# Layer 3's group (1,0): half of its depthwise convolution from VectorE to TensorE, with three small tiles put into one ring

## The chip, the cores and the metric

The kernel runs on one NeuronCore of a Trainium2 chip. TensorE (PE) multiplies matrices, VectorE (DVE) and ScalarE (ACT) work element by element, GpSimd (POOL) does small element work and issues indirect DMAs, SyncE (SP) issues the other DMAs. Each engine runs its own instructions in order, and waits for others by semaphores. The metric is the device time of one execution in microseconds; lower is better.

## The reference, cut to what matters

The input x is 16 images of 192 channels and 32x32 pixels. Four layers each add something to x: `x = x + layer(groupnorm(x))`, with 32 groups of channels.

- Layer 0 is an mLSTM block with a convolution (the kernel's phase A).
- Layer 1 is an attention whose scores come from small simulated quantum circuits: per head a state vector of 64 amplitudes goes through two fixed matrices, and its squares give queries and keys.
- Layer 2 computes offsets with a 3x3 convolution, samples x at the offset positions (9 taps, bilinear), and weights the taps by channel.
- Layer 3 is the one that the change is about:

```
h  = einsum('bchw,oc->bohw', x, w_in)             # 192 -> 510 channels
h  = irfft2(rfft2(2x2 patches of h) * fft_w)      # 2x2 spectral weights
d  = depthwise 3x3 convolution, 510 -> 1020 channels (two outputs per input channel), padding 1
x1, x2 = d[:, :510], d[:, 510:]
y  = einsum('bchw,oc->bohw', gelu(x1) * x2, w_out)
```

## The kernel before

**Phases.** Phase A (layer 0) is one long stage. Phase B holds layers 1 to 3 and the end of layer 0. It is written as five generators that a helper `weave` interleaves by costs that the generators yield: `vectors` (state vectors of layer 1), `attention`, `offsets` and `gathers` (layer 2), and `layer3`. The streams run staggered over the 16 images, so that at any time several images are under way. A scheduler then orders the instructions of each engine, and buffers of a tag are reused in turn (a ring), so that a tile waits until the last reader of the tile that had its buffer is done.

**Layer 3.** The 510 channels are two halves, ab = 0 and 1 (the result of ab=0, `dv[0]`, goes through GELU; that of ab=1, `dv[1]`, is the factor), each in two parts of 128, gt = 0 and 1. For each gt, `rows_in` makes the input rows with TensorE (`phad`, line 1523) and combines them on VectorE into `g.pad` (line 1535); `planes` forms the sums and differences of neighbouring columns, `oe` (line 1571) and two more planes of `pad` (lines 1577 and 1580). Then for eo = 0, 1, the two outputs of an input channel, comes the depthwise convolution, for both ab. So there are eight groups (ab, gt, eo).

A group on VectorE goes by `step`: 12 taps over four planes (a fast form of the 3-tap row filter), of which the first two are ScalarE's (line 1598), ten are VectorE's (line 1600), and between them are one subtraction (line 1616) and one more step (line 1618). A group on TensorE goes by `conv`: for each of the two column halves, nine matrix products of `oe` with diagonal 128x128 matrices (`g.dtaps`, one for each tap; line 1561), summed in PSUM (`pdc`), and one ScalarE eviction (line 1563). `onpe` says for which (gt, eo) the half ab=1 goes to TensorE: (0,0) for images 0 to 13; all four pairs for the last two images. Then come the GELU (ScalarE, line 1625), the product with the other half (line 1627), the output product `pout` (line 1639), and `total`, which loads the residual into `xo` (line 1630), adds (line 1632) and stores (line 1633).

**The diagonal matrices** of (0,0) are built at phase B's start, nine ScalarE instructions on the identity matrix; those that are missing for the last two images are built at image 14, into borrowed `v4` buffers (line 1548).

**Small tiles.** `psit` is a ring of two 2 KB buffers for transposed state vectors `psiT` (line 1084; read by `pcirc`, line 1091). `xp` is a ring of two 2 KB buffers for `ot` (line 1392, offsets), `x2` (lines 1448 to 1457, residual of layer 2) and `xo`. `pos`, `fi`, `fl`, `iv` (lines 1399 to 1417) are single buffers for sampling positions, from which the gather indices `ix` come. `mr` and `mp` (lines 1227 to 1232) are single buffers for row maxima of the attention, which go through DRAM (`mxd`) into `qT`.

Of the kernel before, what the change touches and what calls it, by code (L numbers as in the profile page):

```python
# [10 lines left out]
F32 = mybir.dt.float32  # L11
I32 = mybir.dt.int32
BF16 = mybir.dt.bfloat16
AF = mybir.ActivationFunctionType
ALU = mybir.AluOpType
# [6 lines left out]
HS = 512  # L22
# [782 lines left out]
def phase_b(tc, d, out, ydram, stats, cn, nb):  # L805

    nc = tc.nc
    with ExitStack() as ctx:
# [20 lines left out]
        def sb(tag, bufs, n=HW):  # L829
            return lambda name: p2.tile([128, n], F32, tag=tag, name=name, bufs=bufs)  # L830

        v4, e4, u4 = sb("v4", 5), sb("e4", 3), sb("u4", 3)
        u8 = sb("u8", 2, 2048)
        psit, xp, u384 = sb("psit", 2, HS), sb("xp", 2, HS), sb("u384", 2, 384)

        def pairs(name):
            return p2.tile([128, 2, 192], F32, tag=name, name=name, bufs={"acc": 3, "xt": 2}[name])
# [25 lines left out]
        nc.sync.dma_start(boff, d["b_off"].partition_broadcast(128).rearrange("q n o -> q (n o)"))  # L863
        nc.vector.tensor_tensor(gridb, gridb, boff.unsqueeze(1).to_broadcast([128, 8, 18]), ALU.add)

        wdw = wp.tile([128, 24, 4], F32, name="wdw")
        nc.sync.dma_start(wdw[:, :, 0:3], d["w_dw"].rearrange("p (n x) -> p n x", x=3))
        nc.vector.tensor_copy(wdw[:, :, 3], wdw[:, :, 2])
        wraw = wp.tile([128, 24, 3], F32, name="wraw")
        nc.vector.tensor_copy(wraw, wdw[:, :, 0:3])  # L870
        dtaps = {}
        for gt, eo in ((0, 0),):
            t = wp.tile([128, 9, 128], F32, name=f"dtap{gt}{eo}")
            dtaps[gt, eo] = [t[:, i, :] for i in range(9)]
            for i in range(9):
                nc.scalar.activation(t[:, i, :], cn.ident, AF.Copy,
                                     scale=wraw[:, ((2 + gt) * 2 + eo) * 3 + i // 3, i % 3:i % 3 + 1])
        wa, wb, wc, wd = (wdw[:, :, i] for i in range(4))
        nc.vector.tensor_add(wc, wa, wd)
        nc.vector.tensor_add(wb, wb, wc)  # L880
# [113 lines left out]
def vectors(g, b, left):  # L994
# [82 lines left out]
    for pr in range(3):  # L1077
        ps = []
        for hf in range(2):
            pt = mm("ppsi")  # L1080
            for j in range(4):
                nc.tensor.transpose(pt[:, j * 128:(j + 1) * 128], psi[:, hf * 4 + j, :], cn.ident)
            ps.append(g.psit("psiT"))
            nc.scalar.activation(ps[hf], pt, AF.Identity)
            yield 2.0
        prob = {}
        for w in range(2):
            for hf in range(2):

                pc = big("pcirc")  # L1090
                beside(g.tc, [lambda hh=hh, r=slice(hh * 64, hh * 64 + 64): nc.tensor.matmul(
                    pc[:, hh * HS:(hh + 1) * HS], cn.lqk[r, w, :], ps[hf][r, :], start=True, stop=True)
                    for hh in range(2)])
                prob[w, hf] = v4("prob")
                nc.scalar.activation(prob[w, hf], pc, AF.Square)  # L1095
                yield 2.0

        pz = mm("pz")
        for hh in range(2):
            o = 20 - (pr * 2 + hh) * 4  # L1100
            beside(g.tc, [lambda w=w, hf=hf, q=(w * 2 + hf) * 32: nc.tensor.matmul(
                pz[q:q + 32, :], g.amat[:, w, o:o + 32], prob[w, hf][:, hh * HS:(hh + 1) * HS],
                start=(hh == 0), stop=(hh == 1)) for w in range(2) for hf in range(2)])
        yield 3.0
        if pr == 0:
            nc.scalar.activation(zr, pz, AF.Identity, bias=g.projb)
        else:
            nc.vector.tensor_tensor(zr, zr, pz, ALU.add)
        if pr < 2:
            psi = products(pr + 1)  # L1110
        yield 2.0
# [46 lines left out]
def attention(g):  # L1158
# [14 lines left out]
    def largest(i):  # L1173


        b, pr = pairs[i]
        assert g.done[1] > b
        parts, vo = left[b].parts, g.vo[i % 2]
        kT, qT = g.kt_[i % 2], g.qt_[i % 2]
        xn = g.v4("xn")[:64]  # L1180
        for n, c in ((64, heads[pr][0] * 32),) if pr < 2 else ((32, 64), (32, 160)):
            nc.sync.dma_start(xn[(c == 160) * 32:(c == 160) * 32 + n], g.xnd[b, c:c + n, :])
        for hh in range(2):
            h, o = heads[pr][hh], hh * 64
            for j in range(3):
                key = parts[:, j, 0:480].rearrange("p (t h c) -> p t h c", t=8, h=6)[:, :, h, :]
                diff = parts[:, j, 480:600].rearrange("p (t h c) -> p t h c", t=4, h=6)[:, :, h, :]
                nc.scalar.copy(g.kp[:, :, o:o + 45].rearrange("p t (i j c) -> p t i j c", i=3, j=3)[:, :, :, j, :],
                                      key[:, :, 5:10].unsqueeze(2).to_broadcast([128, 8, 3, 5]))
                nc.scalar.copy(g.kdp[:, :, o:o + 45].rearrange("p t (i j c) -> p t i j c", i=3, j=3)[:, :, :, j, :],  # L1190
                                      diff.unsqueeze(2).to_broadcast([128, 4, 3, 5]))
                nc.scalar.copy(g.qp[:, :, o:o + 45].rearrange("p t (i j c) -> p t i j c", i=3, j=3)[:, :, j],
                                      key[:, :, 0:5].unsqueeze(2).to_broadcast([128, 8, 3, 5]))
        yield 2.0
        rows_of(g.kp, kT)
        rows_of(g.kdp, g.kd)
        rows_of(g.qp, qT)
        yield 3.0
        pv = g.mm("pv").rearrange("p (t h e) -> p t h e", t=8, h=2)
        for tt in range(8):  # L1200
            nc.tensor.transpose(pv[:, tt].rearrange("p h e -> p (h e)"), xn[:, tt * 128:(tt + 1) * 128],
                                cn.ident[:64, :64])
        nc.scalar.activation(vo, pv.rearrange("p t h e -> p t (h e)"), AF.Copy, scale=row("gate"))
        yield 2.0
        mx = p2.tile([128, 2, 8], F32, tag="mx", name="mx")
        for tt in range(8):
            pd, pm = None, None
            for src in (g.kd, kT):
                pm = big("pmax")
                beside(g.tc, [lambda hh=hh, r=slice(hh * 64, hh * 64 + 64): nc.tensor.matmul(  # L1210
                    pm[:, hh * HS:(hh + 1) * HS], qT[r, tt * 128:(tt + 1) * 128], src[r, 0:HS],
                    start=True, stop=True) for hh in range(2)])
                if pd is None:
                    pd, up = pm, e4("up")
                    nc.scalar.activation(up, pd, AF.Relu)  # L1215
                    yield 1.2
            for hh in range(2):
                s = slice(hh * HS, (hh + 1) * HS)
                nc.vector.tensor_tensor_reduce(up[:, s], pm[:, s], up[:, s], 1.0, -3e38, ALU.add, ALU.max,  # L1219
                                               mx[:, hh, tt:tt + 1])  # L1220
            yield 1.2

        yield 1.2
        yield 1.2
        pm = g.mm("pmq")
        nc.tensor.transpose(pm[:16, 0:128], mx.rearrange("p h t -> p (h t)"), cn.ident)
        mr = p2.tile([16, 128], F32, tag="mr", name="mr", bufs=1)
        nc.scalar.activation(mr, pm[:16, 0:128], AF.Identity, scale=-1.0)
        mp = p2.tile([16, 3, 128], BF16, tag="mp", name="mp", bufs=1)
        thirds(nc.vector, mr, [mp[:, j, :] for j in range(3)])  # L1230
        for hh in range(2):
            nc.sync.dma_start(g.mxd[i, hh].rearrange("j (t n) -> t j n", t=8), mp[hh * 8:hh * 8 + 8])
        for hh in range(2):
            nc.sync.dma_start(qT[hh * 64 + 45:hh * 64 + 48, :], g.mxd[i, hh])
        yield 1.0
# [104 lines left out]
def layer2_offsets(g, b, left):  # L1340
# [55 lines left out]
        nc.tensor.transpose(pf[:, j * 128:(j + 1) * 128], ot[:, j * 128:(j + 1) * 128], cn.ident)  # L1396
    yield 4.0
    n = 144
    pos = p1.tile([128, n], F32, tag="pos", name="pos")
    pfv = pf.rearrange("p (j k f c) -> p k f j c", j=4, k=2, f=2)  # L1400
    posv = pos.rearrange("p (f j c) -> p f j c", f=2, j=4)
    nc.vector.tensor_tensor(posv, pfv[:, 0, :, :, 0:18], g.gridb.rearrange("p (f j) c -> p f j c", f=2), ALU.add)
    nc.vector.tensor_tensor(posv, pfv[:, 1, :, :, 0:18], posv, ALU.add)
    nc.vector.tensor_scalar(pos, pos, -1.0, 32.0, ALU.max, ALU.min)
    fi = p1.tile([128, n], I32, tag="fi", name="fi")
    nc.vector.tensor_copy(fi, pos)
    fl = p1.tile([128, n], F32, tag="fl", name="fl")
    nc.vector.tensor_copy(fl, fi)
    t1 = p1.tile([128, n], F32, tag="fi", name="t1")
    nc.vector.tensor_tensor(t1, fl, pos, ALU.is_gt)  # L1410
    nc.vector.tensor_sub(fl, fl, t1)
    nc.vector.tensor_sub(pos, pos, fl)
    flv = fl.rearrange("p (n c) -> p n c", c=2)
    iv = p1.tile([128, n // 2], F32, tag="iv", name="iv")
    nc.vector.scalar_tensor_tensor(iv, flv[:, :, 0], 34.0, flv[:, :, 1], ALU.mult, ALU.add)
    ix = p2.tile([128, n // 2], I32, tag="ix", name="ix")
    nc.vector.tensor_scalar_add(ix, iv, 35.0)
# [66 lines left out]
def layer3(g, b, left):  # L1484
# [99 lines left out]
    for gt in range(2):  # L1584
# [6 lines left out]
        for eo in range(2):  # L1591
# [8 lines left out]
                    nc.vector.scalar_tensor_tensor(out, src, w, add, ALU.mult, ALU.add)  # L1600

            half = [[dv[ab][:, c * HS:(c + 1) * HS] for c in range(2)] for ab in range(2)]
            onpe = (gt, eo) in (((0, 0), (0, 1), (1, 0), (1, 1)) if last else ((0, 0),))
            abs_ = range(1) if onpe else range(2)
            for dy in range(3):
                if onpe and dy:
# [180 lines left out]
```

## Time and profile before

| | |
|---|---|
| median of 3 runs | 7750.31 us (7744.7 to 7766.25) |
| the profiled execution's own time | 7759.77 us |
| its span | 7758.0 us |
| granted TensorE clock, mean of the span | 0.915 |
| busy: TensorE, VectorE, ScalarE, GpSimd | 86%, 81%, 55%, 34% of the span |
| L1600, the tap steps on VectorE | 1060 instructions, 778.2 us |
| L1561, the products of `conv` | 792 instructions, 362.7 us |
| chain that ended last, shares of the span | DVE 21%, PE 15%, issue 11%, DMA 7%, POOL 4%, ACT 3% |

A row of a group reads: line, engine, operation, output<-inputs, shape, count | busy time, mean ns of one | idle time of the engine before it and what ended most of it. A row of waits reads: engine, instruction and line that waited <- what it waited for: microseconds in total, times, longest. A row of the windows view reads: the stretch, its length, then busy microseconds (and instructions) of PE, of its weight loads (PEld), DVE, ACT and POOL, then the granted TensorE clock, the DMA engines' share and GB/s. An f32 matrix product stands in the trace as two instructions.

### The profile page before, as it was taken

To read this page: it belongs to the slowest core of one execution; us is meant where nothing else is said; L and a number is where in the kernel's file an instruction comes from. 1 tells how busy PE (TensorE), PEld (TensorE's weight loads), DVE (VectorE), ACT (ScalarE), POOL (GpSimd) and SP (SyncE) were. 2 spreads that over 40 slices of the span, in tenths; PEclk is the share of its full clock that TensorE was granted. 3 is DMA by queue.
4 is the path that set the end of the run, shared out by engine and by line. 5 is a ranking of instruction groups with operands and counts; after the bars stand their busy time and mean duration, and the time that the engine had idled before them with its cause. 6 is when DMAs were issued, how large, how long until landed. Compare 5 with 4: busy or idle time off the path is not lost.

```text
span 7758.0 us, 94726 instructions
## 1 busy us (share of the span) xinstructions
PE 6690.9 (86%) x32360; PEld 3024.9 (39%) x32360; DVE 6304.9 (81%) x13587; ACT 4301.3 (55%) x7578; POOL 2640.8 (34%) x2125
## 2 busy tenths in 40 slices
PE   6999999999999994788787888888788888877768
PEld 3555555555555552223233333233233323323233
DVE  8888888888888883357887988998898798888886
ACT  6555555555555452766665665666566566556422
POOL 0111111111111110034645545554554565555562
PEclk9999999999999997898998989998899898888878
DMA  1111111111111112045454455545445444544452
GB/s 63 48 50 46 50 50 52 50 47 55 50 47 51 50 44 57 24 132 172 129 154 148 141 151 162 160 147 151 145 142 155 145 153 150 157 147 131 149 169 80
DMA packets 266577, 815.81 MB, mean 105 GB/s; under 512 B 49579, under 2 KB 129725, under 8 KB 266091
## 3 DMA queue, kind: packets, MB, share of 16 engines
q0 software_dynamic: 92160, 453.06, 19.0%
q1 hardware_dynamic: 173931, 356.69, 14.4%
q8 instruction: 254, 4.16, 0.2%
q14 instruction: 232, 1.90, 0.1%
HBM read 667.33 MB, written 133.88 MB: 103 GB/s over the span
## 4 chain that ended last, share of the span: by engine, by line
DVE 21%; PE 15%; issue 11%; DMA 7%; POOL 4%; ACT 3%; SPq 0%; POOLq 0%; DVEq 0%; ACTq 0%; another core or an unknown queue 0%
DVE dc L1600 4%; DMA gt<-xg,ix 3%; DVE up L1219 3%; DVE gt L1469 3%; PE pav L1250 3%; POOL gt L1438 3%; PE pdc L1561 2%; DVE acc L1472 2%; PE pdef L1478 2%; PE phad L1523 2%; DVE acc L1474 2%; POOL df L1360 1%; PE poffc L1386 1%; PE pscore L1257 1%; DVE gnst L32 1%
## 5 line engine op out<-in xcount | busy, mean ns | idle before, releaser
L1438 POOL DMA_INDIRECT gt<-xg,ix x1152 | 1911.6, 1659 | 1911.2 <-DVE acc L1472 1225.9
L529 POOL COPY qbd<-qT 32x384 f32<-32x384 f32 x512 | 318.5, 622 | 2544.2 <-PE se L561 2442.5
L1261 ACT ACTIVATE pexp<-pscore 128x1024 f32<-128x1024 f32 x768 | 783.7, 1022 | 411.9 <-PE pscore L1257 358.1
L1250 PE MATMUL pav<-pexp,vo 128*32 128x512 f32 x3072 | 884.4, 657 | 18.2 <-ACT pexp L1261 8.2
L1469 DVE SCALAR_TENSOR_TENSOR gt<-gt,w 128x384 f32<-128x384 f32 x1152 | 724.1, 645 | 216.0 <-DMA gt<-xg,ix 212.9
L1250 PE MATMUL pav<-pexp,ones 128*32 128x512 f32 x3072 | 891.5, 656 | 0.0
L1600 DVE SCALAR_TENSOR_TENSOR dc<-pad,wdw,dc 128x512 f32<-128x512 f32 x1060 | 778.2, 776 | 19.9 <-ACT dc L1598 19.2
L1478 PE MATMUL pdef<-acc,ident 128*128 128x384 f32 x1152 | 582.7, 597 | 221.9 <-DVE acc L1474 215.2
L1219 DVE CUSTOM_DVE_ANT_0 up<-pmax,up 128x512 f32<-128x512 f32 x768 | 500.1, 684 | 191.0 <-PE pmax L1210 143.2
L1215 ACT ACTIVATE up<-pmax 128x1024 f32<-128x1024 f32 x384 | 391.5, 1019 | 259.8 <-PE pmax L1210 226.4
L559 ACT ACTIVATE dm<-dm,wtm 128x128 f32<-128x128 f32 x1536 | 491.1, 388 | 76.7 <-DVE dm L515 49.9
L1472 DVE SCALAR_TENSOR_TENSOR acc<-gt,w 128x192 f32<-128x192 f32 x1152 | 462.9, 435 | 4.3 <-PE pdef L1478 4.1
L570 PEld LDWEIGHTS pintra<-v,pt 128*128 128x128 f32 x3072 | 390.6, 192 | 169.5 <-issue 104.3
L1257 PE MATMUL pscore<-qt,kt 64*128 64x512 bf16 x1536 | 332.3, 413 | 101.3 <-DVE mx L1219 36.1
L570 PE MATMUL pintra<-v,pt 128*128 128x33 f32 x3072 | 383.6, 271 | 5.2 <-DVE pt L565 4.8
L1478 PEld LDWEIGHTS pdef<-acc,ident 128*128 128x128 f32 x1152 | 200.5, 212 | 458.7 <-DVE acc L1474 304.0
L1561 PE MATMUL pdc<-oe,dtap 128*128 128x496 f32 (+3 forms) x792 | 362.7, 604 | 6.6 <-DVE oe L1571 6.6
L1474 DVE TENSOR_TENSOR acc<-acc,wdef 128x384 f32<-128x384 f32 x576 | 329.9, 573 | 0.3
L1360 POOL TENSOR_TENSOR df<-xpad 96x324 f32<-96x324 f32 x144 | 185.7, 1289 | 413.5 <-issue 333.4
L565 DVE SCALAR_TENSOR_TENSOR pt<-se,dm 128x512 f32<-128x512 f32 x384 | 262.8, 684 | 77.4 <-PE se L561 75.2
L606 PE MATMUL pconv<-yt,wc 128*128 128x512 f32 x640 | 311.5, 607 | 5.3 <-DVE yt L496 2.2
L1523 PE MATMUL phad<-had,win 96*128 96x256 f32 x1024 | 294.7, 434 | 11.6 <-ACT prob L1095 6.6
(444 smaller groups left out, 14066.3 us busy)
## 6 DMA issues: line engine op xcount, KB each, us to landing
dm<-gd SPq DMA_DIRECT2D x128, 768.0 KB
xg<-xt SPq DMA_DIRECT2D x288, 192.0 KB
gt<-xg,ix POOLq DMA_INDIRECT x1152
xb<-x_in SPq DMA_DIRECT2D x32, 384.0 KB
y<-ydram SPq DMA_DIRECT2D x32, 384.0 KB
x1d<-xb SPq DMA_DIRECT2D x32, 384.0 KB
xnd<-y SPq DMA_DIRECT2D x32, 384.0 KB
x<-x1d SPq DMA_DIRECT2D x32, 384.0 KB
```

Of the source, the lines that this page charges most:

```text
L559: nc.scalar.activation(dm[:, h, :], dm[:, h, :], AF.Exp, bias=wtm[:, c, 64 + h:65 + h])
L570: nc.tensor.matmul(pa[:, hh * 33:hh * 33 + 33], pt[:, h * 128:(h + 1) * 128], v33[:, hh, :], start=True, stop=True)
L1219: nc.vector.tensor_tensor_reduce(up[:, s], pm[:, s], up[:, s], 1.0, -3e38, ALU.add, ALU.max, mx[:, hh, tt:tt + 1])
L1250: beside(g.tc, [lambda q=q, hh=hh, w=w: nc.tensor.matmul(po[0][q * 32:q * 32 + 32], w, pe[:, hh * HS:(hh + 1) * HS], start=(tt == 0), stop ...
L1261: nc.scalar.activation(pe, ps, AF.Exp)
L1438: nc.gpsimd.indirect_dma_start(out=gt, out_offset=None, in_=xg, in_offset=bass.IndirectOffsetOnAxis(ap=ix[:, c:c + 1], axis=0))
L1469: nc.vector.scalar_tensor_tensor(gt[:, 0:384], gt[:, 384:768], w2[:, 1, c:c + 1], gt[:, 0:384], ALU.mult, ALU.add)
L1472: nc.vector.scalar_tensor_tensor(acc[:, j, :], gt[:, 192:384], w2[:, 0, c:c + 1], gt[:, 0:192], ALU.mult, ALU.add)
L1474: nc.vector.tensor_mul(acc, acc, g.wdef[:, t, :].unsqueeze(1).to_broadcast([128, 2, 192]))
L1478: nc.tensor.matmul(po[:, 0:384], cn.ident, acc.rearrange("p j c -> p (j c)"), start=(t == 0), stop=(t == 8))
L1561: nc.tensor.matmul(pix[:, y0:y1, x0:x1], g.dtaps[gt, eo][dy * 3 + dx], v[:, y0 + dy - 1:y1 + dy - 1, x0 + sx:x1 + sx], start=(n == 0), sto ...
L1600: nc.vector.scalar_tensor_tensor(out, src, w, add, ALU.mult, ALU.add)
```

## The change

It has two parts. For images 0 to 13, the half ab=1 of (gt, eo) = (1,0) goes to TensorE as well, with nine more diagonal matrices that stay in SBUF (4608 bytes a partition). And the space comes from small tiles: `psit` is given up and `xp` has three buffers in place of two; `psiT`, the four position tiles (as parts of one) and `mr` with `mp` (as parts of one) are taken from `xp` too. Given up are 4096 + 2016 + 1280 bytes a partition, taken are 2048 + 4608. At image 14, two sets of diagonal matrices are built, not three, in three `v4` buffers, not four.

```diff
--- before.py
+++ after.py
@@ -831,7 +831,7 @@
 
         v4, e4, u4 = sb("v4", 5), sb("e4", 3), sb("u4", 3)
         u8 = sb("u8", 2, 2048)
-        psit, xp, u384 = sb("psit", 2, HS), sb("xp", 2, HS), sb("u384", 2, 384)
+        xp, u384 = sb("xp", 3, HS), sb("u384", 2, 384)
 
         def pairs(name):
             return p2.tile([128, 2, 192], F32, tag=name, name=name, bufs={"acc": 3, "xt": 2}[name])
@@ -863,18 +863,18 @@
         nc.sync.dma_start(boff, d["b_off"].partition_broadcast(128).rearrange("q n o -> q (n o)"))
         nc.vector.tensor_tensor(gridb, gridb, boff.unsqueeze(1).to_broadcast([128, 8, 18]), ALU.add)
 
+        wraw = wp.tile([128, 24, 3], F32, name="wraw")
+        dtaps = {}
+        for key in ((0, 0), (1, 0)):
+            t = wp.tile([128, 9, 128], F32, name=f"dtap{key[0]}{key[1]}")
+            dtaps[key] = [t[:, i, :] for i in range(9)]
         wdw = wp.tile([128, 24, 4], F32, name="wdw")
         nc.sync.dma_start(wdw[:, :, 0:3], d["w_dw"].rearrange("p (n x) -> p n x", x=3))
+        nc.vector.tensor_copy(wraw, wdw[:, :, 0:3])
+        for gt, eo in dtaps:
+            for i, t in enumerate(dtaps[gt, eo]):
+                nc.scalar.activation(t, cn.ident, AF.Copy, scale=wraw[:, ((2 + gt) * 2 + eo) * 3 + i // 3, i % 3:i % 3 + 1])
         nc.vector.tensor_copy(wdw[:, :, 3], wdw[:, :, 2])
-        wraw = wp.tile([128, 24, 3], F32, name="wraw")
-        nc.vector.tensor_copy(wraw, wdw[:, :, 0:3])
-        dtaps = {}
-        for gt, eo in ((0, 0),):
-            t = wp.tile([128, 9, 128], F32, name=f"dtap{gt}{eo}")
-            dtaps[gt, eo] = [t[:, i, :] for i in range(9)]
-            for i in range(9):
-                nc.scalar.activation(t[:, i, :], cn.ident, AF.Copy,
-                                     scale=wraw[:, ((2 + gt) * 2 + eo) * 3 + i // 3, i % 3:i % 3 + 1])
         wa, wb, wc, wd = (wdw[:, :, i] for i in range(4))
         nc.vector.tensor_add(wc, wa, wd)
         nc.vector.tensor_add(wb, wb, wc)
@@ -1080,7 +1080,7 @@
             pt = mm("ppsi")
             for j in range(4):
                 nc.tensor.transpose(pt[:, j * 128:(j + 1) * 128], psi[:, hf * 4 + j, :], cn.ident)
-            ps.append(g.psit("psiT"))
+            ps.append(g.xp("psiT"))
             nc.scalar.activation(ps[hf], pt, AF.Identity)
             yield 2.0
         prob = {}
@@ -1224,9 +1224,10 @@
         yield 1.2
         pm = g.mm("pmq")
         nc.tensor.transpose(pm[:16, 0:128], mx.rearrange("p h t -> p (h t)"), cn.ident)
-        mr = p2.tile([16, 128], F32, tag="mr", name="mr", bufs=1)
+        space = g.xp("mr")
+        mr = space[:16, 0:128]
         nc.scalar.activation(mr, pm[:16, 0:128], AF.Identity, scale=-1.0)
-        mp = p2.tile([16, 3, 128], BF16, tag="mp", name="mp", bufs=1)
+        mp = space[:16, 128:320].bitcast(BF16).rearrange("p (j n) -> p j n", j=3)
         thirds(nc.vector, mr, [mp[:, j, :] for j in range(3)])
         for hh in range(2):
             nc.sync.dma_start(g.mxd[i, hh].rearrange("j (t n) -> t j n", t=8), mp[hh * 8:hh * 8 + 8])
@@ -1396,22 +1397,19 @@
         nc.tensor.transpose(pf[:, j * 128:(j + 1) * 128], ot[:, j * 128:(j + 1) * 128], cn.ident)
     yield 4.0
     n = 144
-    pos = p1.tile([128, n], F32, tag="pos", name="pos")
+    space = g.xp("pos")
+    pos, fi, fl, iv = (space[:, o:o + m] for o, m in ((0, n), (n, n), (2 * n, n), (3 * n, n // 2)))
     pfv = pf.rearrange("p (j k f c) -> p k f j c", j=4, k=2, f=2)
     posv = pos.rearrange("p (f j c) -> p f j c", f=2, j=4)
     nc.vector.tensor_tensor(posv, pfv[:, 0, :, :, 0:18], g.gridb.rearrange("p (f j) c -> p f j c", f=2), ALU.add)
     nc.vector.tensor_tensor(posv, pfv[:, 1, :, :, 0:18], posv, ALU.add)
     nc.vector.tensor_scalar(pos, pos, -1.0, 32.0, ALU.max, ALU.min)
-    fi = p1.tile([128, n], I32, tag="fi", name="fi")
-    nc.vector.tensor_copy(fi, pos)
-    fl = p1.tile([128, n], F32, tag="fl", name="fl")
-    nc.vector.tensor_copy(fl, fi)
-    t1 = p1.tile([128, n], F32, tag="fi", name="t1")
-    nc.vector.tensor_tensor(t1, fl, pos, ALU.is_gt)
-    nc.vector.tensor_sub(fl, fl, t1)
+    nc.vector.tensor_copy(fi.bitcast(I32), pos)
+    nc.vector.tensor_copy(fl, fi.bitcast(I32))
+    nc.vector.tensor_tensor(fi, fl, pos, ALU.is_gt)
+    nc.vector.tensor_sub(fl, fl, fi)
     nc.vector.tensor_sub(pos, pos, fl)
     flv = fl.rearrange("p (n c) -> p n c", c=2)
-    iv = p1.tile([128, n // 2], F32, tag="iv", name="iv")
     nc.vector.scalar_tensor_tensor(iv, flv[:, :, 0], 34.0, flv[:, :, 1], ALU.mult, ALU.add)
     ix = p2.tile([128, n // 2], I32, tag="ix", name="ix")
     nc.vector.tensor_scalar_add(ix, iv, 35.0)
@@ -1600,7 +1598,7 @@
                     nc.vector.scalar_tensor_tensor(out, src, w, add, ALU.mult, ALU.add)
 
             half = [[dv[ab][:, c * HS:(c + 1) * HS] for c in range(2)] for ab in range(2)]
-            onpe = (gt, eo) in (((0, 0), (0, 1), (1, 0), (1, 1)) if last else ((0, 0),))
+            onpe = (gt, eo) in (((0, 0), (0, 1), (1, 0), (1, 1)) if last else ((0, 0), (1, 0)))
             abs_ = range(1) if onpe else range(2)
             for dy in range(3):
                 if onpe and dy:
```

## The prediction

> **Durations and base.** Durations are of the one profiled execution: 7759.8 us, of which 7758.0 are the span. The median of the three runs is 7750.3, 9.5 lower, so I work a change out in microseconds and take it from the median. 0.3% (23 us) is about what a measurement of this kernel can tell from no change.
>
> **What bounds the kernel now.** First the page's busy times and its forty slices, to place the change.
>
> ```profile
> PE 6690.9 (86%) x32360; PEld 3024.9 (39%) x32360; DVE 6304.9 (81%) x13587; ACT 4301.3 (55%) x7578; POOL 2640.8 (34%) x2125
> ...
> PE   6999999999999994788787888888788888877768
> ...
> DVE  8888888888888883357887988998898798888886
> ...
> PEclk9999999999999997898998989998899898888878
> ```
>
> Phase A (slices 1 to 16) is TensorE's, at 9 tenths. Everything that the diff touches runs in phase B, from about 3200 us. There neither engine is full: in the steady part the windows view gives
>
> ```profile
> 4000.00:7000.00 3000.00, 2502.37 (x12970) 933.32 (x12967) 2650.88 (x5660) 1862.49 (x2949) 1591.44 (x1085) 0.89 0.49 149
> ```
>
> (columns: stretch, length, busy PE, PEld, DVE, ACT, POOL, then granted clock). The 33 row-maxima steps in it are 11 images, so an image takes 272.7 us, with VectorE busy 241 and TensorE 227. An average hides stages, so I cut one image at layer 3's milestones: A from the last `oe` plane of gt=0 to the GELU of group (0,0); B to the last `oe` plane of gt=1 (group (0,1), then the next `rows_in` and `planes`); C to the GELU of (1,0); D to the GELU of (1,1); E to the next image's planes (`pout`, `total`, the next image's start).
>
> ```profile
> 4808.50:4836.00 27.50, 27.50 (x110) 11.89 (x110) 22.82 (x53) 9.63 (x15) 9.57 (x5) 0.94 0.39 123
> 4836.00:4907.70 71.70, 59.88 (x333) 21.09 (x329) 70.82 (x158) 56.01 (x86) 36.66 (x22) 0.93 0.47 144
> 4907.70:4956.30 48.60, 36.84 (x206) 14.95 (x202) 45.74 (x72) 31.49 (x49) 36.18 (x38) 0.82 0.46 145
> 4956.30:5000.50 44.20, 41.57 (x268) 13.10 (x263) 42.03 (x94) 26.96 (x33) 32.35 (x14) 1.00 0.46 139
> 5000.50:5080.20 79.70, 63.85 (x327) 25.95 (x320) 68.38 (x162) 46.79 (x92) 28.46 (x24) 0.91 0.64 193
> ```
>
> Over nine images the picture repeats. A (mean 27.0 us) is full on TensorE: it holds the group that is on TensorE already. B (72.4) is VectorE's, 98% busy. C (50.9), which holds the group that moves, has VectorE at 94% in the row above and TensorE at 76%, with the lowest clock, 0.82. D (44.5) has both at 93%. E (81.8) has both near 82%, and DMA waits. So the change takes work from the fuller engine of C and gives it to the emptier one.
>
> **The move, part by part.** These rows have the prices:
>
> ```profile
> L1600 DVE SCALAR_TENSOR_TENSOR dc<-pad,wdw,dc 128x512 f32<-128x512 f32 x760 | 559.1, 777 | 1.2 <-ACT dc L1598 0.8
> ...
> L1561 PE MATMUL pdc<-oe,dtap 128*128 128x496 f32 (+3 forms) x792 | 362.7, 604 | 6.6 <-DVE oe L1571 6.6
> ```
>
> *VectorE.* Half ab=1 of group (1,0) leaves: 4 + 6 tap steps (L1600) at 0.777, one subtraction (L1616) at 0.68, one L1618 at 0.79: 9.24 us an image. Images 14 and 15 had it on TensorE before, so 14 change: 129 us.
>
> *ScalarE.* Two first taps (L1598, 0.717 each) leave, two evictions (L1563, 0.596) come: nothing.
>
> *TensorE.* Two `conv` calls an image, nine products each, and every f32 product is two passes in the trace: the page's 792 passes are 44 calls. 362.7 / 44 = 8.24 us a call, 16.5 an image, 231 us in all. So 1.8 us of TensorE pay for 1 us of VectorE. Weight loads could make it dearer: 18 passes load 18 times, at a median of 190 ns. The chain has a row for that, a stretch of 72 passes at the end of the kernel with nothing between:
>
> ```profile
> 7707.75 32.49 PE pdc L1561 x72
> ```
>
> 0.451 us a pass, loads included; the loads lie under the products, and 8.24 stands. [...]
>
> *What fits into C.* TensorE's busy time in C is 37.2 us of 50.9 on average, so 13.7 are idle. Where TensorE runs without a gap its clock is higher: A's nine instances average 0.93, C's 0.81. At A's clock the same 37.2 would take 37.2 x 0.81 / 0.93 = 32.4, 4.8 less. Room: 13.7 + 4.8 = 18.5, against 16.5 needed. On VectorE's side C could shrink by 9.24, on TensorE's by the 2.0 that are left. The smaller one counts: 2.0 x 14 = 28 us. [...] With no such gain the room would be 13.7 and C would lose 2.8 an image.)
>
> In the built program's order A and B keep their work, C and D lose VectorE steps (gather steps of D: 12 to 6; its row maxima almost all go) and E receives them (20 to 24 gather steps, 10 to 18 maxima). So what is late next is E: 66.7 us of VectorE in 81.8 must take in more, and it can only because E's idle 15 us are waits for DMAs (`gt`, `xo`, `x`) that other work may fill. I count that at nothing; if it isn't filled, C's gain goes there, which is the rivals' ground.
>
> *The ring.* 19 tiles an image now go through three slots of `xp`: 6 `psiT`, 4 `x2`, 4 `xo`, 3 `mr`, 1 `ot`, 1 `pos`. In emission order each waits for the tile three places before it. I set the times of one image (4860 to 5045) against that: psiT at 4869.9 follows an `mr` stored at 4862.5, 7 us earlier; `ot` at 4977.7 an `x2` stored at 4959.6; psiT at 4982.7 an `mr` stored at 4964.6; the closest is `pos`, which in the built order takes the slot of `mr`, 20 us free. What would wait in each case is ScalarE, VectorE or SP, with `pexp` or the tap steps queued behind it. For the ring speaks this:
>
> ```profile
> DVE xo L1632 <- DMA xo<-x3d: 36.3, 15, 5.8
> ```
>
> 3.3 us an image, in which `xo` came late since two slots made its load wait for the last `out` store (SP waits 96.0 us in all for that). The third slot should remove some. Bounds: -3.3 an image (-46 us) to +3 (+42, a wait of that size turned the other way, since before has no row for a shared slot). With margins of 7 us and more I take 0.
>
> *The rest.* `pos`, `fi`, `fl`, `iv` as parts of one tile, and `mr` with `mp`: the same instructions, 0. Nine more diagonal builds at phase B's start and nine fewer at image 14 (0.29 us each on ScalarE): -2.6 and +2.6, 0; one `v4` buffer more stays free in the last two images, 0 to -10 us, taken as 0.
>
> Sum: -28 us: 7722, 0.37% under the median.
>
> **Rivals.**
> 1. *VectorE really bounds C and D* (for: 94 and 93% busy; B at 98%, next to C, can hand work into C). Then up to the whole 9.24 is saved, -129 us: 7621; half of it 7686. Against: D's TensorE is at 93%, so the gap that VectorE leaves has TensorE behind it.
> 2. *Slower: TensorE's room in C is not usable.* Three of nine instances of C (58.5, 59.5 and 55.1 us long) hold a long wait of TensorE for POOL's differences:
>
> ```profile
> PE pxt L1376 <- POOL df L1361: 76.0, 25, 15.9
> ```
>
> The other six average 47.5 us with 36.8 busy: 10.7 of room. With half of the clock's gain (2.4) that is 13.1, and C grows by 3.4: 48 us, 7798; without it by 5.8: 81 us, 7831. It decides wherever room falls under 16.5, and shows as ScalarE's `pexp` waiting for `pscore` behind blocks of nine products.
> 3. *The ring costs.* One wait of 3 us an image: +42, 7792.
> 4. *Nothing to see:* E gives back what C saves: 7750.
>
> **Chances.** The forecast's case, -23 to -60 us: 0.27. Rival 1 beyond that: 0.19. Within 23 us (rival 4): 0.20. Rival 2: 0.27. Rival 3: 0.07. Faster 0.46, same 0.20, slower 0.34. The range: 7640 (rival 1 at 85%) to 7805 (rival 2 at +55, a little over its price with half of the clock's gain); some 4% lie under and 9% over it. The forecast's own range, -60 to -23, is 7690 to 7727.
>
> **What would show it.** VectorE's busy time in phase B falls by 129, TensorE's rises by less than 231, with C's clock over 0.90 (right) or still near 0.82 (rival 2). C is shorter than 50.9 and E not longer than 81.8. `xo`'s waits go under 3 us an image; waits of `psiT`, `mr` or `pos` for a DMA or for `pcirc` would be the ring's. I am wrong if C takes 53 us or more, or if E grows by what C loses.

## The result, and the profile after

The kernel after takes **7859.5 us** (median of 4 runs, 7855.2 to 7867.6) against 7753.3 for the kernel before in the same session: ratio 1.013, 95% interval 1.0109 to 1.0151. It is slower by 106 us; the forecast was 28 us faster, and the range ended at 7805. The profiled execution has a span of 7858.2 us, 100.2 over before's 7758.0, and all explanations below are made against that.

The busy times and the forty slices of the kernel after (page, parts 1 and 2):

```profile
PE 6839.6 (87%) x32864; PEld 3101.1 (39%) x32864; DVE 6241.8 (79%) x13419; ACT 4309.0 (55%) x7585; POOL 2378.0 (30%) x2125
...
PE   6999999999999995888888888888888888888868
...
DVE  8888878888888873477898797897898788788886
...
PEclk9999999999999996998999899888998898898978
```

Phase B has become flatter for TensorE (8 in nearly every slice) and VectorE shows 7s where it had 8s and 9s. More work on TensorE and less on VectorE was intended; that the span grew says that the one cost more than the other brought. The groups show both at their prices (page, part 5):

```profile
L1467 DVE SCALAR_TENSOR_TENSOR gt<-gt,w 128x384 f32<-128x384 f32 x1152 | 748.2, 664 | 349.5 <-DMA gt<-xg,ix 348.1
...
L1598 DVE SCALAR_TENSOR_TENSOR dc<-pad,wdw,dc 128x512 f32<-128x512 f32 x920 | 679.6, 771 | 17.4 <-ACT dc L1596 17.2
...
L1559 PE MATMUL pdc<-oe,dtap 128*128 128x496 f32 (+3 forms) x1296 | 593.7, 604 | 8.4 <-DVE oe L1569 6.9
```

The lines have moved by two: L1598 was L1600 (1060 tap steps, now 920), L1559 was L1561 (362.7 us, now 593.7), L1467 was L1469. What has changed beyond the move is the last column of L1467, the first step of a gather's sum: VectorE stands idle 348.1 us in all because the gathered rows have not landed. The same group on the page of before has 212.9:

```profile
L1469 DVE SCALAR_TENSOR_TENSOR gt<-gt,w 128x384 f32<-128x384 f32 x1152 | 724.1, 645 | 216.0 <-DMA gt<-xg,ix 212.9
```

The stretches A to E of one image, cut as in the prediction, in the windows view of after:

```profile
4842.70:4870.50 27.80, 27.80 (x99) 12.56 (x98) 21.38 (x48) 8.90 (x14) 7.81 (x4) 0.88 0.31 91
4870.50:4942.80 72.30, 59.82 (x340) 21.70 (x339) 71.77 (x160) 56.58 (x87) 35.32 (x22) 0.95 0.48 148
4942.80:4975.60 32.80, 28.07 (x117) 11.77 (x114) 32.79 (x54) 18.50 (x29) 23.52 (x24) 0.90 0.45 139
4975.60:5017.60 42.00, 30.01 (x174) 11.29 (x176) 34.18 (x56) 19.86 (x30) 20.64 (x21) 0.84 0.43 137
5017.60:5131.40 113.80, 95.90 (x522) 35.48 (x514) 82.64 (x199) 67.49 (x118) 36.52 (x29) 0.91 0.50 154
```

C is 33 us long, E 114. Means of the 3rd to 13th image, before and after: A 25.6 and 28.5, B 73.6 and 72.3, C 50.7 and 33.3, D 44.2 and 41.2, E 81.0 and 111.0. C and D together lost 20.4 us, more than forecast, and E took all of it and 10 more. An image is 11.3 us longer; the 11 make 124 us, of which the images at both ends give back 24: that is the loss. The stages no longer hold the same work, as the rows show. C ends with the GELU of (1,0), which needs half ab=0 alone and now comes sooner, so other work falls behind it. TensorE's busy time over the same 11 images went from 36.9 to 28.5 us in C (12.7 of the 28.5 are products of the group that moved), from 40.5 to 31.8 in D, and from 66.2 to 93.0 in E.

What waited, in the waits of 4000 to 7000 us; first before, then after:

```profile
DVE gt L1469 <- DMA gt<-xg,ix: 99.7, 49, 9.6
...
PE pdef L1478 <- DVE acc L1474: 125.8, 68, 6.3
...
PE pscore L1257 <- DVE mx L1219: 18.5, 14, 4.3
```

```profile
DVE gt L1467 <- DMA gt<-xg,ix: 223.2, 124, 7.5
...
PE pscore L1258 <- DVE mx L1219: 120.4, 36, 8.3
...
PE pdef L1476 <- DVE acc L1472: 37.3, 33, 4.5
```

Two waits have grown by 124 and 102 us in 3000: VectorE for gathers, TensorE for the row maxima. A third has shrunk by 88: TensorE for VectorE's sums of the gathers (`pdef`). How the two that grew can hang together is seen in one place of the timeline of after, at the second `conv` call of (1,0) (start, duration, engine, line; idle time before in brackets). TensorE:

```profile
4971.23 7.67 PE L1559 MATMUL pdc<-oe,dtap 128*128 128x512 f32 x18
...
4979.17 0.39 PE L1210 MATMUL pmax<-kt,qt 64*128 64x512 bf16 x2
...
4986.67 0.61 PE L1258 MATMUL pscore<-qt,kt 64*128 64x512 bf16 x2 [5.44 <-DVE mx L1219]
```

and VectorE at the same time:

```profile
4980.19 0.62 DVE L1467 SCALAR_TENSOR_TENSOR gt<-gt,w 128x384 f32<-128x384 f32 x1 [1.38 <-DMA gt<-xg,ix]
4982.63 0.68 DVE L1467 SCALAR_TENSOR_TENSOR gt<-gt,w 128x384 f32<-128x384 f32 x1 [1.83 <-DMA gt<-xg,ix]
4983.23 2.16 DVE L1598 SCALAR_TENSOR_TENSOR dc<-pad,wdw,dc 128x512 f32<-128x512 f32 x2
4985.32 0.68 DVE L1219 CUSTOM_DVE_ANT_0 up<-pmax,up 128x512 f32<-128x512 f32 x1
```

The block of 18 passes holds TensorE for 7.67 us; `pmax` is behind it. VectorE has come to its gather steps before their data (3.2 us of waiting at the head of its queue), and the row maxima (`up`, `mx`, L1219) are queued behind those. TensorE then stands 5.44 us until `mx` is there. This is one place; that the loss comes about in this way is not shown by it.

### The profile page after: what moved, and what is told of

Its sections match the earlier page's. It is cut to its first block, busy times and chain, and to the rows that moved or that the text cites. A ratio compares the mean times of both kernels' runs of the same rounds, so it can differ in the third digit from the quotient of the medians.

```text
span 7858.2 us, 95761 instructions
## 1 busy us (share of the span) xinstructions
PE 6839.6 (87%) x32864; PEld 3101.1 (39%) x32864; DVE 6241.8 (79%) x13419; ACT 4309.0 (55%) x7585; POOL 2378.0 (30%) x2125
## 5 line engine op out<-in xcount | busy, mean ns | idle before, releaser
L1436 POOL DMA_INDIRECT gt<-xg,ix x1152 | 1679.1, 1458 | 2263.2 <-DVE acc L1470 1350.4
L1467 DVE SCALAR_TENSOR_TENSOR gt<-gt,w 128x384 f32<-128x384 f32 x1152 | 748.2, 664 | 349.5 <-DMA gt<-xg,ix 348.1
L1598 DVE SCALAR_TENSOR_TENSOR dc<-pad,wdw,dc 128x512 f32<-128x512 f32 x920 | 679.6, 771 | 17.4 <-ACT dc L1596 17.2
L1219 DVE CUSTOM_DVE_ANT_0 up<-pmax,up 128x512 f32<-128x512 f32 x768 | 499.4, 683 | 243.0 <-PE pmax L1210 187.8
L1559 PE MATMUL pdc<-oe,dtap 128*128 128x496 f32 (+3 forms) x1296 | 593.7, 604 | 8.4 <-DVE oe L1569 6.9
L1559 PEld LDWEIGHTS pdc<-oe,dtap 128*128 128x128 f32 x1296 | 244.8, 197 | 288.7 <-issue 263.0
L1258 PEld LDWEIGHTS <-kt 64*128 64x128 bf16 x1536 | 87.6, 94 | 624.7 <-issue 602.8
```

The costliest lines, as they stand in the source:

```text
L1436: nc.gpsimd.indirect_dma_start(out=gt, out_offset=None, in_=xg, in_offset=bass.IndirectOffsetOnAxis(ap=ix[:, c:c + 1], axis=0))
L1467: nc.vector.scalar_tensor_tensor(gt[:, 0:384], gt[:, 384:768], w2[:, 1, c:c + 1], gt[:, 0:384], ALU.mult, ALU.add)
L1559: nc.tensor.matmul(pix[:, y0:y1, x0:x1], g.dtaps[gt, eo][dy * 3 + dx], v[:, y0 + dy - 1:y1 + dy - 1, x0 + sx:x1 + sx], start=(n == 0), sto ...
```

## The experiments

Medians are of four or more runs; the kernel before took 7757 to 7763 us beside them. All ratios are against it.

**1. The ring or the group?** `ring_only` is the kernel after without group (1,0), `group_only` the tiles of before with it:

```diff
 ring_only:   onpe = (gt, eo) in (... if last else ((0, 0),))          # the ring of 3 stays
 group_only:  dtaps[gt, eo] = dtaps[1, 0] = [t[:, i, :] for i in range(9)]
              onpe = (gt, eo) in (... if last else ((0, 0), (1, 0)))   # the tiles of before stay
```

> The ring of three as in the changed kernel, but only group (0,0) on TensorE, as before. Theory 1 (TensorE's queue: the 16.5 us of products of group (1,0) stand ahead of layer 2's transposes pxt and its offset products poffc, so the indices ix come late and the gathers run dry): within 20 us of before, 7735 to 7775, and from C's start to ix about 87 us as before. Theory 2 (the ring: ot, psiT and mr are placed or wait behind each other's slots, which makes ix late): at least 40 us slower than before, over 7795, with ot some 8 us after the last poffc.

> Group (1,0) on TensorE for all images, but with the separate small tiles of before; for want of space group (1,0) uses the diagonals of (0,0), so its numbers are wrong and its instructions the same. Theory 1: 7815 to 7865, like the changed kernel. Theory 2: no slower than before, 7620 to 7765.

`ring_only` 7780.9 us, ratio 1.0024 (1.0006 to 1.0043); `group_only` 7885.5, 1.0168 (1.0141 to 1.0195). The group alone makes the loss. The ring costs 24 us alone and gains 26 beside the group (7885.5 to 7859.5): small, and its sign depends on what else is there. But look at the two waits in `ring_only`, 4000 to 7000 us:

```profile
DVE gt L1467 <- DMA gt<-xg,ix: 170.5, 81, 6.9
...
PE pscore L1258 <- DVE mx L1219: 75.4, 28, 5.8
```

Both have more than half of their growth already (99.7 and 18.5 before), although VectorE and TensorE have the work of before, and the kernel loses 24 us only. So these waits go with the change, but their size doesn't measure the loss.

**2. The price of the products and the worth of the relief.** `one_product` is the kernel after with one product for nine in group (1,0); `group01` and `group11` move another group in its place.

```diff
 one_product: if (gt, eo) == (1, 0) and not last:
                  order = order[:1]
 group01, group11:  ... if last else ((0, 0), (0, 1))    and    ((0, 0), (1, 1))
```

> The changed kernel with one product (the middle tap) in place of nine in each call of conv for group (1,0), images 0 to 13: VectorE is relieved all the same, TensorE pays about 2 us an image in place of 16.5. Leaves eight taps of that group out. Theory 1: the loss goes and VectorE's relief shows, 7640 to 7740. Theory 2: still slower than before, over 7790. A third theory (it is VectorE's own shorter row that reorders the work so that gathers are used up too early) also says over 7770, with ix as late as in the changed kernel.

> As the changed kernel, but with group (0,1) as the second on TensorE in place of (1,0), with its own diagonals. Its products lie in B, where VectorE is 98% busy and layer 2's transposes are not yet due. Theory 1: C's start to ix about 87 us, B shorter than 72, 7650 to 7740. Theory 2: over 7790, since the ring is the same. If TensorE as a whole is the bound, it is as slow as the changed kernel, 7830 to 7880.

> As the changed kernel, with group (1,1) as the second on TensorE in place of (1,0), with its own diagonals. Theory T: the place is second to the amount, 7840 to 7960. If the place decides (products ahead of layer 2's transposes in C are the harm), D comes after most of them: under 7800.

`one_product` 7712.9 us, 0.9943 (0.9922 to 0.9963); `group01` 7964.1, 1.0271 (1.0243 to 1.0299); `group11` 7902.1, 1.0178 (1.0148 to 1.0208). So the products left out cost 147 us (7859.5 - 7712.9). VectorE's relief nearly without them is worth 44 against the kernel before (7757 - 7713), and 68 against `ring_only` (7780.9), which has the same ring: a third to a half of its 129. The loss adds up as +24 for the ring, -68 for the relief, +147 for the products. The gather wait in `one_product`:

```profile
DVE gt L1467 <- DMA gt<-xg,ix: 201.0, 108, 7.2
```

201.0 us in 3000, at 276.0 an image, are 18.5 an image; before has 99.7 x 277.0 / 3000 = 9.2. The wait has grown by 9.3, and the work that left VectorE was 9.24, but that the one became the other is not shown: `ring_only`, with nothing taken off VectorE, has 15.9 already (at 279.7 an image). VectorE's idle time in all is 36.3 us an image in `one_product`, 35.1 in `ring_only` and 32.2 before. The other two groups cost more than (1,0), not less: no place within layer 3 was better.

**3. Is one engine simply the bound?** Less, more, and no work of group (0,0) on TensorE, in the kernel before:

```diff
 one_product_00: if not last: order = order[:1]
 twice_00:       if not last: order = order * 2
 no_group:       ... if last else ()
```

> The kernel before, with one product in place of nine in each conv call of group (0,0), images 0 to 13 (eight taps are left out): TensorE has some 14.6 us less an image, VectorE the same work. Theory T (TensorE is the bound of the steady part although it shows only 83 to 84% busy: it was so in the four kernels run so far, whatever VectorE had): an image gets shorter by most of 14.6 / 0.84, 7530 to 7640. Theory V (VectorE at 88% is the bound, and the loss of the changed kernel comes from where its products stand): no more than 30 us under before, 7720 to 7775.

> The kernel before, with each conv call of group (0,0) summing its nine products twice (18 products, so its value is doubled), images 0 to 13: TensorE has 16.5 us more an image, VectorE the same. Theory T: as dear as nine more products were in the changed kernel against its version with one (147 us for 14 images) or dearer, 7880 to 8000. Theory V: the products lie in A, which no layer-2 transposes share, so under 7820.

> The kernel before with no group on TensorE for images 0 to 13: TensorE 16.5 us less an image, VectorE 9.2 more (252 of 275). Theory T: TensorE alone would allow 255 us an image, VectorE then stops it near 262 to 272, 7580 to 7740: a version faster than both. Theory V: slower than before by what VectorE's 9.2 us cost, at least the 44 us that one product's run gained, 7795 to 7890.

`one_product_00` 7802.9 us, 1.0046 (1.0019 to 1.0072); `twice_00` 7821.0, 1.0073 (1.0049 to 1.0096); `no_group` 7915.2, 1.0187 (1.0152 to 1.0221). Neither less nor more is faster. A kernel that TensorE bounds would have gained from `one_product_00`, one that VectorE bounds would have stayed as it was in `twice_00`. Both theories as I had put them fall (T and V in the expectations). That group (0,0) on TensorE is worth some 155 us (`no_group`), while (1,0) costs 106, says that it is not the amount of work alone.

**4. The place in TensorE's queue.** In TensorE's order of the kernel after, the two blocks of (1,0) stand ahead of and among layer 2's `pxt`, with `poffc` behind, and between the steps of a row maximum. The streams are woven by starts and rates, so one number moves the blocks, and all of layer 3 with them, without changing any work; `spread` leaves the start as it is and cuts the blocks.

```diff
-               (gathers(g), 120.0, 2.91), (stream(3, layer3), 136.9, 3.96)])
+               (gathers(g), 120.0, 2.91), (stream(3, layer3), 136.9, 4.06)])   # late10; late20 4.16
 spread:  after products 3 and 6 of a call: yield 1.2   (in place of 3.6 behind the call)
```

> The kernel after with layer 3 begun 0.20 of an image later (4.16 for 3.96), all else the same. In its order the 18 products of group (1,0) stand behind layer 2's offsets (after the last poffc and poff), no longer ahead of pxt and poffc. Theory O (the loss is the place: two blocks of 8.2 us ahead of pxt and poffc delay the chain offsets, ix, gathers): the steady period comes back from 286 to about 275 us or less, and against the kernel before begun equally late the group gains or costs nothing (difference under 40 us). Theory W (some 16 us of TensorE cost 8 to 11 us of an image wherever they stand, since the image is a chain that passes from engine to engine): the difference between this run and the kernel before begun equally late stays near 100 to 150 us.

> The control: the kernel before with layer 3 begun 0.20 of an image later, nothing else changed. What it differs from before is the price of the later start alone: theory O expects little in the period (275 us) and up to 55 us at the end of the kernel, where the last image's layer 3 comes later; theory W has no number for it. The pair late20 minus this one is the price of group (1,0) at its other place.

> The kernel after with layer 3 begun 0.10 of an image later: the first block of nine products stands between the poffc, behind all pxt. Theory O: the end of poffc comes back from 81 towards 70 us after layer 3's milestone is corrected for the shift, the period to about 278 us, 7750 to 7800 us in all. Theory W: as after, 7850 us or more.

> The kernel after with the nine products of a call handed out in three parts of three, so that pxt, pscore and pav stand between them; same products, same start of layer 3. If it is the lump (a block of 8.2 us that nobody can pass) that delays pxt and pscore, a good part of the 100 us comes back: 7760 to 7810 us. If it is the amount of TensorE ahead of poffc (theory O by quantity, or theory W), the time stays within 25 us of after's 7860.

`late20` 7874.5 us, 1.0148 (1.0105 to 1.0192); `before_late20` 7913.0, 1.0189 (1.0146 to 1.0233): the later start costs both, but with the group on TensorE the kernel is now 38 us *faster*, and the runs of the two do not overlap (7866 to 7883, 7899 to 7928). `late10` 7768.6, 1.0015 (0.9994 to 1.0036): 91 us come back. `spread` 7932.3, 1.0226 (1.0183 to 1.0269): cutting the blocks makes it worse. The edit cuts the calls of (0,0) too, and other work of the order moves with it, so it gives the lump no support but doesn't rule it out. In `late10` the two waits read:

```profile
DVE gt L1467 <- DMA gt<-xg,ix: 174.1, 100, 6.3
...
PE pscore L1258 <- DVE mx L1219: 27.9, 22, 3.9
```

The wait for row maxima is back near before's 18.5, the wait for gathers is not.

**5. Is it the place, or is the later start a better schedule for any version?** Controls, two more places, the ring taken out, and the products taken out at the new place:

```diff
 before_late05, before_late10:  the kernel before, start 4.01, 4.06
 late05, late15:                the kernel after, start 4.01, 4.11
 group_only_late10, one_product_late10:  those of 1 and 2, start 4.06
```

> The kernel before with layer 3 begun 0.10 of an image later, nothing else. Theory O (the place of the products in the chain pxt, poffc, ix): the later start brings nothing by itself, 7750 to 7800 us, so that at this start the change costs under 20 us or gains. Rival S (the later start is a better schedule for any version): 7650 to 7690 us, and the change still costs some 80 to 110 us at this start.

> Group (1,0) on TensorE in the tiles of before, layer 3 begun 0.10 later: late10 without the ring. At the old start the ring made 18 to 26 us of difference in either direction (ring_only 24 over before, group_only 26 over after). If the ring is worth nothing, 7750 to 7790 us as late10; a third slot that helps would show as 20 us or more over late10.

> The kernel after with layer 3 begun 0.05 of an image later: the first block of nine products stands just behind the last but one pxt group and ahead of poffc, the second within poffc. Theory O: between late10's 7769 and after's 7860, nearer to late10, since only one block is ahead of poffc and none among the earlier pxt: 7780 to 7820 us.

> The kernel after with layer 3 begun 0.15 of an image later: the first block stands near the end of poffc, the second behind it, ahead of poff. Theory O alone would have it at or under late10, 7740 to 7780 us; but the start of 4.16 took 7874 and its control 7913, so the later start has a price of its own, and the time may lie between, 7770 to 7870 us.

> late10 with one product for nine in group (1,0)'s two calls for images 0 to 13 (the other products of that group are left out, so its output is not the reference's). At the old start this saved 147 us. Theory O (the price is that of the place): it saves less than 75 us here, 7695 to 7765. Theory W (TensorE's work costs the same wherever it stands, and the later start gained by something else): it saves about 150 us again, near 7620.

> The kernel before with layer 3 begun 0.05 of an image later, nothing else. Between before (7760) and before_late10 (7745), so that the change costs 60 to 75 us at this start (late05 took 7820): the price falls step by step as the blocks move behind pxt and poffc. Under 7740 it would be the fastest version seen.

| start | kernel before | kernel after | the change costs |
|---|---|---|---|
| 3.96 | 7753.3 | 7859.5 | +106 |
| 4.01 | 7692.1, 0.9918 (0.9893 to 0.9944) | 7820.1, 1.008 (1.0052 to 1.0107) | +128 |
| 4.06 | 7745.1, 0.9984 (0.9971 to 0.9998) | 7768.6 | +24 |
| 4.11 | not run | 7875.0, 1.016 (1.0129 to 1.019) | |
| 4.16 | 7913.0 | 7874.5 | -38 |

`one_product_late10` took 7695.9, 0.9923 (0.9894 to 0.9953): at 4.06 the same products cost 73 us where they cost 147 at 3.96. `group_only_late10` took 7800.5, 1.0053 (1.0033 to 1.0073), 32 more than `late10`: here the ring helps. The relief, by the comparison that gave 44 at 3.96, is worth 49 there (7745.1 to 7695.9). So layer 3's start sets the price: the same 18 products and the same relief cost from +128 to -38 us. But the price does not fall step by step as I expected: `before_late05` gained 65 us, which I had not foreseen, `late05` kept the full price, and `late15` lies above its range. The start moves the kernel before as well, by 221 us from its best to its worst, more than it moves the kernel after (106): the -38 stands where both are slow. That it is the place of the two blocks in TensorE's queue, and not how all streams meet, is not shown. The fastest version found is `before_late05`, 7692.1 us: a start 0.05 later, with the group left on VectorE. It beats both kernels.

An image's account, from one last `ix` to the next over 11 images, shows what differs between the pairs (us; the gather wait is that of 4000 to 7000, scaled to an image):

| kernel | image | TensorE busy | idle | VectorE busy | idle | of it for gathers |
|---|---|---|---|---|---|---|
| before | 277.0 | 230.7 | 46.3 | 244.8 | 32.2 | 9.2 |
| after | 288.7 | 242.4 | 46.3 | 240.7 | 48.0 | 21.5 |
| before_late05 | 273.9 | 232.0 | 41.9 | 245.2 | 28.7 | 5.1 |
| late05 | 286.3 | 247.2 | 39.1 | 241.1 | 45.2 | 15.4 |
| before_late10 | 278.9 | 234.7 | 44.2 | 242.4 | 36.5 | 9.0 |
| late10 | 281.6 | 244.7 | 36.9 | 237.8 | 43.8 | 16.3 |
| before_late20 | 293.0 | 237.6 | 55.4 | 244.5 | 48.5 | 21.7 |
| late20 | 290.5 | 244.9 | 45.6 | 236.9 | 53.6 | 21.9 |

At 3.96 TensorE's idle time is 46.3 before and 46.3 after: of the room that the forecast counted on, nothing was used, and the image grew by exactly what TensorE's busy time grew (11.7). At the later starts TensorE's idle time fell by 2.8, 7.3 and 9.8 us, against 15.2, 10.0 and 7.3 of added busy time. What is left is the cost an image: 11.7, 12.4, 2.7 and -2.5. The wait for gathers that the change brings falls too, 12.3, 10.3, 7.3 and 0.2, but not in step, and it doesn't set the time: `late15` has 10.8 of it at 290.5 an image, half of what the kernel after has, and is no faster (7875.0).

## Why the prediction was wrong, step by step

- **The prices were right.** TensorE: 593.7 - 362.7 = 231.0 us, as forecast to the microsecond; a pass stayed at 604 ns. The weight loads don't show as idle time: the 1296 of L1559 took 244.8 us (197 ns each), and the row of its products has 8.4 us idle ahead of them, 6.9 of it a wait for `oe`. VectorE: 140 tap steps (113.1, count times mean) and 28 steps of L1616 and L1618 in the kernel before's lines (16.0) left, 129 together.
- **The busy times followed only in part.** TensorE's rose by 148.7 and not 231: the rest got shorter (6328.2 to 6245.9 us), which goes with a higher clock (0.894 to 0.902 an image). VectorE's fell by 63.1 and not 129: its other instructions got longer (gather steps L1467 by 24.1 us), and its records overlap less (added up singly they fell by 115).
- **"What fits into C" is the step that failed.** Its signs came true and told nothing of the time: C's clock went to 0.94 on average, over the 0.90 that was to show it right, and C shrank by 17 us. But the sum added 16.5 us to a C whose work was to stay (37.2 us of TensorE), and it did not stay: C holds 28.5 with the products in it, and TensorE's busy time in E grew by 26.8. And the idle time of a stage was taken for room. It was time in which TensorE waited for others; with the products there, one wait fell (`pdef` for VectorE's sums: 125.8 to 37.3 us) and another rose (`pscore` for `mx`: 18.5 to 120.4). The idle time of the whole image did not fall at all (46.3 and 46.3). The clock's gain was local as well: while C's rose from 0.81 to 0.94, D's fell from 0.96 to 0.85 and A's from 0.94 to 0.91. Nor is the clock highest where TensorE has no gap: in the rows of after above, A is busy for 27.80 of 27.80 us at 0.88, B for 59.82 of 72.30 at 0.95.
- **"What is late next is E", counted at nothing, was the other failure.** The prediction said that E's gather waits might be filled by the work pushed into it, and that C's gain would go there if not. It went there, and more: E's gather waits did not fill, they went from 6.4 to 16.1 us an image, and VectorE's idle time in E from 15.1 to 30.3 (the same 11 images). Why is open. The tap steps may have covered a gather's way (4.8 us from issue to landing on the page of after) in part: `one_product` has 2.6 us an image more of this wait than `ring_only`. But `ring_only` has 170.5 of the 223.2 us in all with no tap step taken off. "If E grows by what C loses" was one of the two signs named for being wrong, and it is what happened.
- **The ring: 0 was a fair value.** +24 alone, -26 and -32 with the group, all within the bounds of -46 to +42. VectorE's waits of `xo` for its load are gone, as said. SyncE's for the last `out` store ahead of an `xo` load went from 71.7 to 57.1 in 4000 to 7000 us, and of the waits for another tile's store in the ring the engines have only this in that stretch:

```profile
ACT psiT L1084 <- DMA mxd<-mr: 0.8, 3, 0.3
```

- **The rivals.** Rival 2 (TensorE's room is not usable) had the right side and half of the cause, at 48 to 81 us; it still took 10.7 to 13.1 us of C's idle time for room, and looked for the growth in C, which shrank. Rival 1 (VectorE bounds): with the products nearly gone the relief brought 44 to 68 us in `one_product`, about its half and not the whole 129; with the products in, nothing of it was left. Rival 4 (E gives back what C saves) had the place, and too small a size.
- **A smaller slip.** The prediction's 272.7 us an image divides a fixed 3000 us by 11 steps that don't fill it; from `ix` to `ix` an image takes 277.0, with 230.7 of TensorE and 244.8 of VectorE. No term of the sum hangs on it.
- **What stays open.** That the products cost more than the relief brings, and that layer 3's start sets the price, is shown. The route (a block ahead of `pmax`, gather steps ahead of `mx`, then `pscore`) is read from one place of the trace, and it can't be the only one: in `late05` the wait of `pscore` for `mx` is only 22.7 us in the same stretch and the change still costs 128. Why `one_product_00` and `no_group` are slower with less work on TensorE isn't settled either.

## What to carry to other kernels

Where two engines are each 80 to 90% busy and hand work to each other, an idle share in one stage need not be room: ask of each microsecond of it what the engine is waiting for, and whether that will come earlier when the engine is busy with something else; if not, the added work can cost its full length, as TensorE's 11.7 us an image did here. A wait that grew is not yet the cause: see whether a run that loses little has it too, as `ring_only` does. And before giving up or keeping such a move, shift the whole stage against the others by some per cent of a period in *both* versions: here 5 to 20% moved the price of the same change from +128 to -38 us, and 5% alone, without the change, gave the fastest kernel.

## What the runs showed of the hardware that I had not expected

In `one_product_00` TensorE had less work, and what remained got dearer: 448 passes fewer run and the products' busy time fell by 197.2 us (362.7 to 165.5), 14.1 for each of 14 images, but the granted clock in the image fell from 0.894 to 0.866 (0.851 in `no_group`), and TensorE's busy time an image went down only from 230.7 to 222.1; `twice_00` has 0.910. The windows view of 4000 to 7000 us, `no_group` first and then `late10`:

```profile
4000.00:7000.00 3000.00, 2286.74 (x11883) 853.63 (x11883) 2599.44 (x5519) 1769.75 (x2805) 1623.83 (x1025) 0.85 0.46 142
```

```profile
4000.00:7000.00 3000.00, 2606.42 (x13163) 1000.46 (x13161) 2531.26 (x5432) 1864.46 (x2928) 1330.77 (x1078) 0.91 0.48 147
```

The columns are those of the prediction: TensorE busy 76% at a clock of 0.85, and 87% at 0.91. What lowered the clock in the runs with less work is not shown.
